# A chunked log-linear attention and gated FFN kernel: exponent rows in two fp16 parts, another order of the first transfers, and another list of due times

## The chip, the cores and the metric

One core of a Trainium2 chip runs the whole program. The metric is device time in microseconds (us), the median of several executions. Engines are called PE (TensorE, matmuls), DVE (VectorE), ACT (ScalarE), POOL (GpSimd) and SP (the queue from which all transfers are issued).

## The reference, cut to what matters

The input x is (2, 2048, 256), fp32: B = 2 sequences of T = 2048 tokens, D = 256. Layer 1 is attention with 16 heads of 64 key and 16 value dimensions, a decay and a level-dependent weight:

```
Q, K, V = x @ Wq.T, x @ Wk.T, x @ Wv.T;  dl = x @ Wdl.T        # 16 heads, 12 levels
g   = -exp(A_log) * softplus(x @ Wdt.T + dt_bias)
Lam = softplus(Lp * dl);  cg = cumsum(g, axis=time)
decay[t,s] = exp(cg[t] - cg[s])  for s <= t, else 0
lam[t,s]   = Lam[t, level(t,s)]   # level: 0 if s == t, else floor(log2(s xor t)) + 1
W = (Q K^T / 8) * decay * lam;   o = (W V) @ Wout.T + x
attention = layernorm(o) * ln_g + ln_b
x = layernorm(x + attention)
```

Layer 2 is a gated cell that runs over the two sequences as two time steps (c = f*c + i*g with sigmoid, sigmoid, tanh gates), with output h = tanh(x @ wo.T + c_final @ uo.T + bo); the result is layernorm(x + h).

## The kernel before

**Tiling.** The 2048 tokens are cut into 16 blocks of P = 128 (NC = 16); both sequences are handled in one pass over the blocks. Weights and activations are kept as two fp16 parts (names in `_h` and `_l`, or `xth`, `xtl`), so that a product takes three matmuls. For each block c:

- `load_x` brings the transposed block xt and makes xth (a cast) and xtl (the rest).
- `project` makes values, level weights and decays (pv, z, m, u, ln). `gp` holds g in parts; matmuls pc with `tri` and `ones` make its prefix sums. The logarithms of decay and level weight, 10 rows of 16 heads (LL), are split into parts in RP, transposed by PE (pt), copied out (RT), written to DRAM (scr, cg2) and read back as `Rb[b]` (tiles R0 and R1: rows of the query side) and `st[32:]` (rows of the key side, broadcast).
- `keys` makes Q and K (pqk, 8 groups of 12 matmuls), split into F (ACT) and L (DVE).
- `attend` makes the exponents by matmul: `arg = st.T @ Rb` sums, for each key and query, the right rows; ACT's exponential of it, DL, is decay times level weight. Scores sc are multiplied into DL on DVE, pi = DL.T @ V. What lies outside the block comes from up to four stored states (pin, SH, SL); pu and pS make the block's own state.
- `finish` runs po, two layernorms, a transpose (pt_x), the gates gt, pcu, ph, tanh, the last layernorm (hh) and the store. The last block (`fine`) does this one sequence at a time, with `warm` matmuls in between.

**Three bf16 parts.** Each exponent row is held as three bf16 numbers that sum to it: 30 rows, one for masked entries (-1e30) and an empty one make 32 rows a sequence, 64 in all with 16 heads (8 transposes of 128 columns). The arg matmuls contract 128 rows: 32 of indicators and query rows, 96 of the key side (2 x 48).

**The order of the work.** Every operation goes through a `Recorder`. `add` notes it with an estimated duration (`cost`); `depend` finds what each must wait for; `order` then plans: it steps through time with the estimated durations, numbers of buffers (`BUFS`) and of PSUM banks (`BANKS`), and on each engine starts, of the operations that are ready, the one with the earliest due time (`late`). `issue` emits the plan, and each engine runs its list strictly in that order. All instructions thus come from one line, L536, and are told apart by their tiles. Before, due times come from a due time for each block's output (`DUE`), followed backwards through the durations, plus a bias for each kind of operation (`BIAS`); `FIRST` names the first 16 transfers in order:

```
late[i] = min([outs.get(i, 1e9)] + [late[s] - ops[i].dur - ops[i].lat for s in succ[i]])
late = [x + bias.get(o.kind, bias.get(o.kind.split("@")[0], 0.0)) for x, o in zip(late, ops)]
late = [o.rank - 1e6 if o.rank >= 0 else x for x, o in zip(late, ops)]
```

Of the kernel before, what the change touches and what calls it, by code (L numbers as in the profile page):

```python
# [22 lines left out]
P = 128  # L23
# [3 lines left out]
NEG = -1e30  # L27
EPS = 1e-5
PERM = [3, 4, 5, 6, 7, 8, 9, 10, 11, 0, 1, 2]
SW = 64.0  # L30


DUE = [
    2677.57, 7721.13, 18978.35, 19716.23, 26604.1, 27450.81, 30772.73, 32390.67,
    34188.43, 36425.9, 37687.87, 40156.28, 43733.31, 46896.49, 47598.73, 59076.43,
]
BIAS = {
    'DVE:id16': -544.41, 'POOL:mhalf': -2585.45, 'POOL:ones': -884.87, 'POOL:RP': 1536.59, 'DMA:xt32@0': -4046.65,
    'DVE:xth@0': 1406.88, 'POOL:xtl@0': -518.54, 'DMA:xn@0': -2368.1, 'DMA:LpB@0': -3281.08, 'POOL:LpB@0': 860.85,
    'DVE:LpB@0': -244.97, 'DMA:bc_dtb@0': -2440.29, 'DMA:stg_wv@0': -6352.72, 'ACT:wv_h@0': -1203.55,  # L40
    'DVE:wv_l@0': 268.05, 'DMA:bc_Alog@0': -6629.31, 'ACT:bc_Alog@0': -1742.76, 'DVE:bc_Alog@0': -856.29,
    'DMA:mk@0': -4013.56, 'DMA:tri@0': -3595.99, 'DMA:stg_wq@0': -3921.89, 'ACT:wq_h@0': -1587.01,
    'DVE:wq_l@0': 1004.73, 'DMA:stg_wk@0': -4796.3, 'ACT:wk_h@0': 1541.09, 'DVE:wk_l@0': 3050.85,
    'DMA:st@0': -6284.79, 'DMA:R0@0': -6277.05, 'DMA:R1@0': -5991.07, 'POOL:SH@0': 665.45, 'POOL:SL@0': -2142.9,
    'POOL:VZ0@0': 1168.73, 'POOL:VZ1@0': -2626.46, 'PE:pv@0': -2541.05, 'DVE:z@0': -3273.44, 'ACT:VZ0@0': -4024.21,
    'POOL:z@0': -405.5, 'DVE:m@0': 572.33, 'ACT:u@0': 300.83, 'ACT:ln@0': 419.02, 'DVE:u@0': -1545.81,
    'ACT:LL@0': -482.21, 'POOL:g@0': -945.72, 'POOL:gp@0': 847.34, 'POOL:gr@0': 2525.08, 'PE:pc@0': -832.96,
    'POOL:LL@0': -1927.28, 'POOL:lf@0': -892.19, 'DVE:RP@0': 1443.6, 'DVE:r1@0': -759.26, 'PE:pt@0': -4539.93,
    'ACT:RT@0': -4433.14, 'DMA:scr@0': -628.34, 'DMA:cg2@0': -2529.67, 'POOL:E@0': -1904.15, 'ACT:E@0': -1974.72,
    'POOL:wv@0': 181.98, 'PE:pqk@0': 64.39, 'ACT:F@0': 1604.82, 'DVE:L@0': 240.14, 'DMA:bc_lng@0': 2134.89,  # L50
    'DMA:bc_lnb@0': -3284.28, 'DMA:bc_bo@0': 2756.69, 'DMA:ic@0': 2678.73, 'DMA:fb@0': 1506.14,
    'DMA:stg_wo@0': 214.04, 'ACT:wo_h@0': 749.49, 'DVE:wo_l@0': 13.57, 'DMA:stg_fw@0': 1917.56,
    'ACT:fw_h@0': -4483.73, 'DVE:fw_l@0': 3214.87, 'DVE:ich@0': 420.52, 'DVE:icl@0': -4538.93, 'PE:pg@0': 1562.45,
    'DVE:gb@0': 1718.11, 'PE:pu@0': 476.98, 'ACT:Uh@0': 2949.46, 'DVE:Ul@0': 1151.14, 'PE:pS@0': 1579.04,
    'ACT:N0@0': -3364.34, 'POOL:Ne0@0': -1812.42, 'POOL:Nt0@0': 2666.57, 'PE:arg@0': 1940.26, 'ACT:DL@0': 617.53,
    'PE:sc@0': 1032.21, 'DVE:DL@0': -2154.89, 'PE:pi@0': 14.24, 'ACT:YT@0': -2007.66, 'DVE:YTl@0': -1029.9,
    'ACT:SH@0': -122.62, 'DMA:xc@0': -943.46, 'PE:po@0': 1994.93, 'DVE:o@0': 25.16, 'POOL:xc@0': 1259.58,
    'DVE:st6@0': -1858.28, 'DVE:mv@0': -3427.79, 'POOL:rs@0': -1949.61, 'DVE:x1@0': -5553.71, 'PE:pt_x@0': -1400.7,
    'ACT:tr_x@0': -2328.9, 'DVE:tr_x@0': 2309.54, 'PE:gt@0': -1288.93, 'ACT:tg@0': -946.21, 'DVE:ct@0': -235.27,
    'DVE:c20@0': -3271.11, 'ACT:chh@0': -1127.08, 'DVE:chl@0': 554.25, 'DVE:c21@0': -872.21, 'PE:pcu@0': 3059.02,  # L60
    'DVE:cu@0': 1460.37, 'PE:ph@0': 1875.67, 'DVE:hh@0': -3488.44, 'ACT:hh@0': 132.07, 'POOL:hh@0': 3054.19,
    'DMA:out@0': 3049.1, 'DMA:xt32': -1810.23, 'DVE:xth': 64.72, 'POOL:xtl': -114.25, 'DMA:xn': -34.41,
    'PE:pv': -827.63, 'DVE:z': -1783.61, 'ACT:VZ1': -2672.79, 'POOL:z': 778.86, 'DVE:m': -789.82, 'ACT:u': 160.38,
    'ACT:ln': 591.53, 'DVE:u': 565.39, 'ACT:LL': 4374.65, 'POOL:g': 743.3, 'POOL:gp': -706.56, 'POOL:gr': 1663.66,
    'PE:pc': -2010.17, 'POOL:LL': 2926.67, 'POOL:lf': 3821.96, 'DVE:RP': -662.55, 'DVE:r1': -2759.89,
    'PE:pt': -165.69, 'ACT:RT': 659.27, 'DMA:scr': -1065.41, 'DMA:cg2': -986.92, 'DMA:st': 2349.73,
    'DMA:R0': -4459.06, 'DMA:R1': -920.98, 'POOL:E': 164.31, 'ACT:E': 3751.96, 'POOL:wv': -2316.25,
    'PE:pqk': 3231.38, 'ACT:F': 2373.65, 'DVE:L': 1459.54, 'POOL:ca': 2673.82, 'ACT:coef': 777.82,
    'PE:pu': 1486.59, 'ACT:Uh': -1034.21, 'DVE:Ul': -1341.83, 'PE:pS': -1300.83, 'ACT:N1': -1363.27,
    'POOL:Ne1': 3295.45, 'POOL:Nt1': -3412.65, 'POOL:mt': -860.48, 'POOL:N1': 1496.08, 'PE:arg': 10.51,  # L70
    'ACT:DL': -378.27, 'PE:sc': 1271.55, 'DVE:DL': 214.57, 'PE:pi': -1471.85, 'PE:pin': 557.54, 'DVE:Yi': 2234.51,
    'ACT:Yh': 1604.54, 'POOL:Yl': 569.07, 'ACT:YT': -714.54, 'DVE:YTl': -122.31, 'ACT:SH': 3886.77,
    'POOL:SL': -2249.79, 'DMA:xc': 1825.76, 'PE:po': -3323.98, 'DVE:o': -660.15, 'POOL:xc': -169.22,
    'DVE:st6': -348.25, 'DVE:mv': -2225.59, 'POOL:rs': 414.73, 'DVE:x1': -228.81, 'PE:pt_x': -545.23,
    'ACT:tr_x': -194.42, 'DVE:tr_x': 94.93, 'PE:gt': -1722.42, 'ACT:tg': -1182.38, 'DVE:ct': -4965.5,
    'DVE:c20': -807.68, 'ACT:chh': -2859.38, 'DVE:chl': -3393.25, 'DVE:c21': 92.69, 'PE:pcu': -3235.88,
    'DVE:cu': 958.49, 'PE:ph': 1685.23, 'DVE:hh': -2322.3, 'ACT:hh': -1393.34, 'POOL:hh': 1020.15,
    'DMA:out': -1687.37, 'ACT:VZ0': 887.84, 'ACT:N0': -1579.9, 'POOL:Ne0': 662.46, 'POOL:Nt0': 2273.86,
    'POOL:acc0': 1222.8, 'ACT:N2': 2274.54, 'POOL:Ne2': -1305.11, 'POOL:Nt2': 3789.98, 'POOL:N2': -2988.84,
    'DVE:tq': -1338.55, 'POOL:Yi': -418.52, 'POOL:acc1': -4347.71, 'ACT:N3': -1472.76, 'POOL:Ne3': -1671.15,  # L80
    'POOL:Nt3': -1206.59, 'POOL:N3': 747.56, 'DMA:xc@8': 15056.81, 'PE:po@8': 11984.32, 'DVE:o@8': 12872.18,
    'POOL:xc@8': 12701.25, 'DVE:st6@8': 9516.16, 'DVE:mv@8': 11273.9, 'POOL:rs@8': 13415.76, 'DVE:x1@8': 7496.93,
    'PE:pt_x@8': 12669.14, 'ACT:tr_x@8': 11859.29, 'DVE:tr_x@8': 8427.28, 'PE:gt@8': 10079.09,
    'ACT:tg@8': 16255.28, 'DVE:ct@8': 13065.88, 'DVE:c20@8': 12123.56, 'ACT:chh@8': 6769.1, 'DVE:chl@8': 13861.4,
    'DVE:c21@8': 9374.46, 'PE:pcu@8': 9104.07, 'DVE:cu@8': 14670.33, 'PE:ph@8': 10197.25, 'DVE:hh@8': 14713.5,
    'ACT:hh@8': 13013.82, 'POOL:hh@8': 17906.53, 'DMA:out@8': 8066.82, 'DMA:xt32@9': -3472.99,
    'DVE:xth@9': -6943.2, 'POOL:xtl@9': -7979.66, 'PE:pv@9': -7250.49, 'DVE:z@9': -7399.69, 'ACT:VZ1@9': -5093.65,
    'POOL:z@9': -8444.59, 'DVE:m@9': -3821.67, 'ACT:u@9': -8298.34, 'ACT:ln@9': -7589.28, 'DVE:u@9': -8544.13,
    'ACT:LL@9': -4666.75, 'POOL:g@9': -6445.41, 'POOL:gp@9': -525.04, 'POOL:gr@9': 1071.48, 'PE:pc@9': -5094.17,
    'POOL:LL@9': -7512.85, 'POOL:lf@9': -7085.42, 'DVE:RP@9': -8900.61, 'DVE:r1@9': -5745.08, 'PE:pt@9': -6171.97,  # L90
    'ACT:RT@9': -9289.92, 'DMA:scr@9': -5138.62, 'DMA:cg2@9': -12451.75, 'DMA:st@9': -8335.6, 'DMA:R0@9': -4913.0,
    'DMA:R1@9': -1320.23, 'PE:pqk@9': -5086.21, 'ACT:F@9': -2346.26, 'DVE:L@9': -4425.52, 'POOL:ca@9': -1966.77,
    'POOL:acc0@9': -4203.44, 'POOL:acc1@9': -2628.34, 'POOL:acc2@9': -6977.55, 'ACT:coef@9': -5726.39,
    'PE:arg@9': -8364.73, 'ACT:DL@9': -6371.85, 'PE:sc@9': -2442.58, 'DVE:DL@9': -5936.8, 'PE:pi@9': -8104.24,
    'PE:pin@9': -6842.43, 'DVE:Yi@9': -7958.54, 'DVE:tq@9': -4871.42, 'POOL:Yi@9': -9414.91, 'ACT:Yh@9': 923.7,
    'DVE:Yl@9': -13.59, 'ACT:YT@9': -5899.02, 'DVE:YTl@9': 948.32, 'DMA:xc@9': -3131.16, 'PE:po@9': -10407.06,
    'DVE:o@9': -6391.56, 'POOL:xc@9': -5874.17, 'PE:warm@9': 2241.77, 'DVE:st6@9': -3233.97, 'DVE:mv@9': -6158.55,
    'POOL:rs@9': -4272.53, 'DVE:x1@9': -8481.89, 'PE:pt_x@9': -10891.67, 'ACT:tr_x@9': -8747.79,
    'DVE:tr_x@9': -3011.58, 'DVE:b16@9': -459.04, 'PE:ph1@9': 2189.17, 'PE:gt0@9': -1044.0, 'ACT:tg@9': -4313.81,
    'DVE:ct@9': -4064.32, 'DVE:c20@9': -8811.46, 'ACT:chh@9': -9398.28, 'DVE:chl@9': -4364.2, 'PE:gt1@9': -8791.8,  # L100
# [1027 lines left out]
```

## Time and profile before

| what | value |
|---|---|
| median of 3 runs | 614.75 us (614.02 to 618.04) |
| the profiled execution | 615.93 us |
| its span, first to last instruction | 614.1 us |
| granted PE clock, mean | 0.991 |
| busy: PE, DVE, ACT, POOL | 585.6, 502.4, 383.4, 303.5 us |
| moved by DMA | 46.36 MB in 70139 packets |

The profile is one execution. An engine's busy time is the sum of its instructions' durations; PE's matmuls are pipelined, so they overlap and their modelled length is longer than the spacing at which they are issued. PEld is the loading of weights, beside the matmuls. A group's row gives the tiles (output <- input), the shape, the count, busy us, mean ns of one, and then the idle time ahead of it with what ended most of that. PEclk is the clock granted to PE in tenths: it was half until 13.2 us, for 3.4 us from 47.3, and at the very end.

### The profile page before, as it was taken

What the parts mean: (1) busy time and instruction counts of PE and PEld (TensorE: products, weight loads), DVE (VectorE), ACT (ScalarE), POOL (GpSimd) and SP (SyncE); (2) the same over time, 40 slices, a digit from 0 to 9 for tenths busy, and PEclk for the clock granted to TensorE, in tenths of its full rate; (3) what the DMA queues carried; (4) which work ended last, traced back from release to release, by engine and by line L of the source; (5) the groups of instructions that cost most, each with busy time, mean ns of one, the idle gap of its engine ahead of it and who ended that gap; (6) DMA issues with size and microseconds to landing.
All of it is one profiled execution on the core that took longest, in us unless ns stands there. A gap on an engine that the chain in (4) does not pass through costs nothing.

```text
span 614.1 us, 24206 instructions
## 1 busy us (share of the span) xinstructions
PE 585.6 (95%) x10382; PEld 504.2 (82%) x10382; DVE 502.4 (82%) x1196; ACT 383.4 (62%) x914; POOL 303.5 (49%) x666
## 2 busy tenths in 40 slices
PE   5988999999999999999999999999999999999894
PEld 2776788988898788978889888888988889888794
DVE  5977958888879997789786888897978879787974
ACT  4666587465784856558664674857467594664552
POOL 4461646134735729244772464547376455353432
PEclk9998999999999999999999999999999999999997
DMA  8785134311243205041411514114050512203001
GB/s 245 182 189 130 36 73 91 90 35 38 60 101 91 71 3 141 20 108 35 110 36 37 125 37 91 54 25 119 20 141 21 108 37 75 70 4 101 27 2 35
DMA packets 70139, 46.36 MB, mean 75 GB/s; under 512 B 23984, under 2 KB 67760, under 8 KB 70000
## 3 DMA queue, kind: packets, MB, share of 16 engines
q1 hardware_dynamic: 70032, 44.82, 29.3%
q8 instruction: 81, 1.33, 0.9%
q14 instruction: 26, 0.21, 0.1%
HBM read 35.63 MB, written 9.18 MB: 73 GB/s over the span
## 4 chain that ended last, share of the span: by engine, by line
PE 45%; DVE 23%; POOL 13%; ACT 9%; DMA 6%; issue 3%; SPq 0%; POOLq 0%; ACTq 0%; DVEq 0%
PE gt L536 10%; PE pqk L536 9%; PE pi L536 4%; PE sc L536 4%; POOL rs L536 3%; DVE DL L536 3%; PE ph L536 3%; DVE L L536 3%; ACT DL L536 3%; DVE m L536 3%; PE pv L536 3%; PE arg L536 2%; PE pin L536 2%; DVE st L536 2%; PE pu L536 2%
## 5 line engine op out<-in xcount | busy, mean ns | idle before, releaser
L536 PEld LDWEIGHTS <-fw_h 128*128 128x128 f16 x1176 | 90.9, 98 | 5.0 <-ACT fw_h L536 2.0
L536 ACT ACTIVATE F<-pqk 128x512 f16<-128x512 f32 x128 | 73.7, 616 | 30.3 <-PE pqk L536 28.5
L536 DVE SCALAR_TENSOR_TENSOR L<-pqk,F 128x512 f16<-128x512 f32 x128 | 82.6, 676 | 5.9 <-ACT F L536 5.9
L536 DVE SCALAR_TENSOR_TENSOR DL<-sc,DL 128x512 f32<-128x512 f32 x128 | 81.7, 677 | 4.8 <-PE sc L536 3.6
L536 PE MATMUL gt<-tr_x,fw_h 128*128 128x128 f16 x768 | 82.6, 219 | 0.3 <-DVE tr_x L536 0.2
L536 PEld LDWEIGHTS <-wk_h 128*128 128x128 f16 x992 | 69.9, 98 | 6.2 <-issue 0.6
L536 ACT ACTIVATE tg<-gt,gb 128x128 f32<-128x128 f32 x192 | 53.8, 373 | 33.9 <-PE gt L536 33.3
L536 ACT ACTIVATE DL<-arg 128x512 f32<-128x512 f32 x128 | 68.1, 616 | 6.8 <-PE arg L536 6.5
L536 PE MATMUL pqk<-xth,wq_h 128*128 128x256 f16 x256 | 70.1, 274 | 0.3 <-DVE o L536 0.3
L536 PE MATMUL gt<-tr_x,fw_l 128*128 128x128 f16 x384 | 70.0, 219 | 0.0
L536 PE MATMUL pqk<-xtl,wq_h 128*128 128x256 f16 x256 | 70.0, 273 | 0.0
L536 PE MATMUL pqk<-xth,wq_l 128*128 128x256 f16 x256 | 69.9, 273 | 0.0
L536 PEld LDWEIGHTS <-F 64*128 64x128 f16 x2048 | 60.8, 93 | 10.9 <-issue 8.4
L536 PE MATMUL pqk<-xth,wk_l 128*128 128x256 f16 x256 | 69.8, 272 | 0.0
L536 PE MATMUL pqk<-xth,wk_h 128*128 128x256 f16 x256 | 69.8, 272 | 0.0
L536 PE MATMUL pqk<-xtl,wk_h 128*128 128x256 f16 x256 | 69.7, 272 | 0.0
L536 PEld LDWEIGHTS <-fw_l 128*128 128x128 f16 x588 | 57.3, 98 | 1.8 <-DVE fw_l L536 1.0
L536 PEld LDWEIGHTS <-wq_h 128*128 128x128 f16 x512 | 48.6, 98 | 8.0 <-issue 0.7
L536 POOL TENSOR_TENSOR Yi<-Yi,tq 128x256 f32<-128x256 f32 x32 | 25.3, 791 | 49.2 <-DVE Yi L536 33.3
L536 PEld LDWEIGHTS <-wk_l 128*128 128x128 f16 x496 | 46.2, 98 | 4.1 <-issue 1.0
L536 PE MATMUL sc<-F 64*128 64x128 f16 x512 | 46.4, 218 | 0.3 <-DVE L L536 0.3
L536 PEld LDWEIGHTS <-L 64*128 64x128 f16 x1024 | 45.2, 93 | 0.7 <-issue 0.4
(179 smaller groups left out, 1809.7 us busy)
## 6 DMA issues: line engine op xcount, KB each, us to landing
st<-cg SPq DMA_DIRECT2D x16, 768.0 KB, 6.3
xt<-xT SPq DMA_DIRECT2D x16, 256.0 KB, 2.8
xc<-x SPq DMA_DIRECT2D x16, 256.0 KB, 2.8
scr<-RT SPq DMA_DIRECT2D x16, 256.0 KB, 2.9
R<-scr SPq DMA_DIRECT2D x32, 128.0 KB, 2.9
xn<-x SPq DMA_DIRECT2D x15, 256.0 KB, 3.2
out<-hh SPq DMA_DIRECT2D x15, 256.0 KB, 2.2
stg_fw<-fw SPq DMA_DIRECT2D x8, 256.0 KB, 3.7
```

Of the source, the lines that this page charges most:

```text
L536: getattr(eng.real, meth)(*[real(x) for x in a], **{q: real(x) for q, x in k.items()})
```

## The change

It has three parts.

1. *Exponent rows.* RP holds each row as two fp16 parts (20 rows a sequence, 5 transposes in place of 8). `g` is limited from below to -500 (one more POOL operation), split into two fp16 parts in place of three bf16 (4 pc matmuls in place of 6). Masked entries become 32768 x (-60000) through a constant row of `rc`. The DRAM copies shrink with it: cg2 has 32 rows a sequence in place of 48, st[32:96] is filled in place of st[32:128], R is read with 20 rows in place of 32, and arg contracts 96 rows in place of 128. st, R, tri, ones are fp16.
2. *The opening.* The first block's xth is made by ACT and xtl by DVE (before: DVE and POOL); wv arrives as two transfers of half the rows, each converted by itself. SP's first transfers are xt, wv (two), wq, wk, Lp, dtb, Alog, the second halves of wq and wk, tri, mk; before: xt, wv, wq, Lp, dtb, wk, Alog, tri, mk, the second halves.
3. *Due times.* `DUE`, `BIAS` and `FIRST` go. `PLAN` is a string with two characters for each recorded operation, its due time. BUFS, BANKS and some estimates of `cost` change with it. The whole order on every engine is new.

The core of the diff (PLAN's characters left out):

```diff
-NEG = -1e30
+NEG, GMIN = -60000.0, -500.0
...
-BANKS = {'y': 8, 'z': 8, 'x': 4, 'a': 7, 's': 5, 'p': 6, 't': 7,}
-FIRST = ["xt32", "stg_wv", "stg_wq", "LpB", "bc_dtb", "stg_wk", "bc_Alog", "tri", "mk", "xt32", "stg_wq", "stg_wk", "st", "R0", "R1", "xn"]
+BANKS = {'y': 7, 'z': 4, 'x': 4, 'a': 6, 's': 5, 'p': 4, 't': 6,}
...
             if sb > tb:
-                st[30, tb, s] = 1
+                st[20, tb, s] = 32768
                 continue
-            st[27:30, tb, s] = 1
+            st[18:20, tb, s] = 1
             row = (6, 7, 5, 8)[s % 4] if sb == tb else level(4 * tb, 4 * sb) - 3
-            st[3 * row:3 * row + 3, tb, s] = 1
+            st[2 * row:2 * row + 2, tb, s] = 1
...
-        late = [1e9] * n
-        for i in range(n - 1, -1, -1):
-            late[i] = min([outs.get(i, 1e9)] + [late[s] - ops[i].dur - ops[i].lat for s in succ[i]])
-        bias = BIAS
-        late = [x + bias.get(o.kind, bias.get(o.kind.split("@")[0], 0.0)) for x, o in zip(late, ops)]
-        late = [o.rank - 1e6 if o.rank >= 0 else x for x, o in zip(late, ops)]
+        base = len(DIGITS)
+        late = [DIGITS.index(code[2 * i]) * base + DIGITS.index(code[2 * i + 1]) - 200 for i in range(n)]
...
-                SP.dma_start(t, src)
-                act(hi[:, :, c0:c0 + w], t, AF.Copy, scale=SW)
-                V.scalar_tensor_tensor(lo[:, :, c0:c0 + w], t, SW, hi[:, :, c0:c0 + w], ALU.mult, ALU.subtract)
+                for ks in [slice(0, 1), slice(1, 2)] if name == "wv" else [slice(0, 2)]:
+                    SP.dma_start(t[:, ks], src[:, ks])
+                    act(hi[:, ks, c0:c0 + w], t[:, ks], AF.Copy, scale=SW)
+                    V.scalar_tensor_tensor(lo[:, ks, c0:c0 + w], t[:, ks], SW, hi[:, ks, c0:c0 + w], ALU.mult, ALU.subtract)
...
-            V.tensor_copy(xth, xt32)
-            G.tensor_tensor(xtl, xt32, xth, ALU.subtract)
+            if c == 0:
+                act(xth, xt32, AF.Copy)
+                V.tensor_tensor(xtl, xt32, xth, ALU.subtract)
+            else:
+                V.tensor_copy(xth, xt32)
+                G.tensor_tensor(xtl, xt32, xth, ALU.subtract)
...
+            G.tensor_scalar(g, g, GMIN, None, ALU.max)
-            gp, gr = work("gp", [3, B, H], BF16), work("gr", [B, H])
+            gp = work("gp", [2, B, H], F16)
             G.tensor_copy(gp[:, 0], g)
-            G.tensor_tensor(gr, g, gp[:, 0], ALU.subtract)
-            G.tensor_copy(gp[:, 1], gr)
-            G.tensor_tensor(gp[:, 2], gr, gp[:, 1], ALU.subtract)
+            G.tensor_tensor(gp[:, 1], g, gp[:, 0], ALU.subtract)
...
-                for q in range(3):
-                    PE.matmul(pc[:, 32 * j:32 * j + 32], w, gp[:, q].rearrange("p b h -> p (b h)"), start=(q == 0), stop=(q == 2))
+                for q in range(2):
+                    PE.matmul(pc[:, 32 * j:32 * j + 32], w, gp[:, q].rearrange("p b h -> p (b h)"), start=(q == 0), stop=(q == 1))
...
-            r1 = work("r1", [B, 10, H])
-            V.tensor_copy(RPv[:, :, :, 0, :], RF)
-            V.tensor_tensor(r1, RF, RPv[:, :, :, 0, :], ALU.subtract)
-            V.tensor_copy(RPv[:, :, :, 1, :], r1)
-            V.tensor_tensor(RPv[:, :, :, 2, :], r1, RPv[:, :, :, 1, :], ALU.subtract)
-            for q in range(8):
-                PE.transpose(pt[:, q, :], RP[:, q * P:(q + 1) * P], idb)
-            RT = work("RT", [8, P], BF16)
-            act(RT, pt, AF.Copy)
+            V.tensor_copy(RP[:, :, :, 0, :], RF)
+            V.tensor_tensor(RP[:, :, :, 1, :], RF, RP[:, :, :, 0, :], ALU.subtract)
+            for q in range(5):
+                PE.transpose(pt[:, q, :], RPf[:, q * P:(q + 1) * P], idh)
+            RT = work("RT", [5, P], F16)
+            act(RT, pt[:, 0:5, :], AF.Copy)
...
-            SP.dma_start(st[32:].rearrange("k (a d) t -> k a (d t)", d=2),
-                         cg2.rearrange("b k t -> (b k) t").unsqueeze(1).to_broadcast([96, 16, 2 * P]))
+            SP.dma_start(st[32:96].rearrange("k (a d) t -> k a (d t)", d=2),
+                         cg2.rearrange("b k t -> (b k) t").unsqueeze(1).to_broadcast([64, 16, 2 * P]))
...
-                SP.dma_start(Rb[b][:32].rearrange("k h t -> k (h t)"), rows[32 * b:32 * b + 32].rearrange("k h t -> k (h t)"))
+                SP.dma_start(Rb[b][:20].rearrange("k h t -> k (h t)"), rows[b].rearrange("k h t -> k (h t)"))
...
-                        PE.matmul(pa[:, :, 4 * j4:4 * j4 + 4], st[:, tb, :], Rb[b][:, :, 4 * tb:4 * tb + 4],
+                        PE.matmul(pa[:, :, 4 * j4:4 * j4 + 4], st[:96, tb, :], Rb[b][:96, :, 4 * tb:4 * tb + 4],
```

## The prediction

> **What bounds the kernel now.** I read the engine table and the slices first, then a table by stages, then TensorE's waits, then the opening and the single groups that the change touches. All sums are made against the profiled execution: span 614.1 us, 615.93 us with what lies around it, 1.2 us above the median of 614.75.
>
> ```profile
> PE 585.6 (95%) x10382; PEld 504.2 (82%) x10382; DVE 502.4 (82%) x1196; ACT 383.4 (62%) x914; POOL 303.5 (49%) x666
> ...
> PE   5988999999999999999999999999999999999894
> ...
> PEclk9998999999999999999999999999999999999997
> ```
>
> TensorE (PE) is the bound for some 570 us; what it does not do is idle at both ends and in slices 2 to 4. VectorE (DVE) at 82% is no bound, but close enough that a late operation there stalls PE. By stages (columns: length, then busy us and instructions of PE, weight loads, DVE, ACT, POOL; clock; DMA):
>
> ```profile
> 0.00:12.30 12.30, 4.82 (x13) 1.73 (x14) 6.30 (x7) 5.27 (x7) 7.05 (x18) 1.00 0.77 236
> 12.30:30.00 17.70, 17.20 (x174) 13.82 (x173) 16.09 (x32) 11.70 (x25) 7.21 (x22) 1.00 0.78 198
> 30.00:60.00 30.00, 25.61 (x430) 20.79 (x432) 22.37 (x43) 18.05 (x41) 12.31 (x29) 0.94 0.71 167
> 60.00:584.00 524.00, 515.79 (x9495) 447.87 (x9486) 439.29 (x1063) 337.06 (x808) 268.26 (x581) 1.00 0.27 66
> 584.00:614.20 30.20, 22.15 (x289) 20.02 (x286) 18.38 (x55) 11.34 (x36) 8.70 (x17) 0.88 0.06 19
> ```
>
> Busy time flatters PE, because a matmul's modelled length (0.219 us for 128 columns) is four times its spacing in a stream (0.056). So I also took spacings from the trace: 0.109 us for 256 columns, 0.056 for 128, 0.029 for 64, 0.0265 for 32, and 0.095 extra wherever PE goes between whole-array matmuls and the half-height (sc, pin) or quarter-width (pi) ones. What exceeds the spacings I call lost: 11 us before 30, 7.3 from 30 to 60, 14.6 from 60 to 584, and some 10 after. The 14.6 are many short stalls; the largest are of the exponent matmuls arg:
>
> ```profile
> PE arg L536 <- DVE L L536: 2.3, 6, 0.8
> PE pS L536 <- DVE mv L536: 0.7, 1, 0.7
> PE pi L536 <- POOL Yl L536: 0.6, 1, 0.6
> ```
>
> By spacings, 5.8 of the 14.6 us stand in front of an arg group (3.6 between two arg groups, 2.2 between a pqk and an arg group). A group of eight takes PE 0.23 us, its exponential 0.6 us on ACT: PE runs out of banks when such groups are bunched.
>
> **The PE stream.**
>
> ```profile
> L536 PE MATMUL pt<-idb,RP 128*128 128x128 bf16 x128 | 9.8, 220 | 0.7 <-DVE z L536 0.5 <-DVE L L536 0.2
> L536 PE MATMUL arg<-R,st 128*128 128x64 bf16 x1024 | 41.6, 192 | 4.0 <-DVE L L536 2.3 <-ACT DL L536 0.8
> L536 PEld LDWEIGHTS <-st 128*128 128x128 bf16 x1024 | 38.2, 97 | 8.1 <-issue 6.7
> L536 PEld LDWEIGHTS <-L 64*128 64x128 f16 x1024 | 45.2, 93 | 0.7 <-issue 0.4
> ```
>
> Transposes pt go from 8 to 5 a block: 48 x 0.056 = 2.7 us less. Prefix matmuls pc go from 6 to 4: 32 x 0.0265 = 0.8 us less. In the instruction order of the two built programs, changes of array shape rise from 163 to 184: 21 x 0.095 = 2.0 us more. Stream: -1.5 us (range -3.5, if the changes fall into stalls, to -0.5).
>
> The 1024 arg matmuls keep their 64 columns, but contract 96 rows instead of 128, in fp16. No row has 96 rows. Low bound: a load with 64 rows takes 93 ns against 97 with 128, and fp16 streams at the spacing of bf16, so nothing. High bound: each takes the 0.056 us of a 128-column matmul, 1024 x 0.027 = +27.6 us. I take nothing, since 96 rows lie between two heights that behave alike. The Trainium skill, "TensorE: Matmul & The Clock Gate", section "LDWEIGHTS (loading the stationary operand)", says that loading time follows the columns and not the rows; by it the term is nothing too, and no run here shows 96 rows.
>
> **Other engines, per block.** DVE loses a cast and a subtraction around r1 (0.390 + 0.551 us by their groups): 15 us in all. ACT's copy RT shrinks from 1024 to 640 columns (1.03 to about 0.65 us): 6 us; table loads go from 28 to 24 at 1.283 us: 5.1 us. POOL swaps a cast and a subtraction (0.23 + 0.25) for one tensor_scalar (0.36 by Nt's row): 2 us. DMA: the broadcast into st falls from 768 to 512 KB, scr from 256 to 160, the two R loads from 128 to 80 each: 0.45 MB a block. None of it is PE time; the cover is PE's own queue. With the cover gone, the path from m to the first arg would be 1.5 us shorter, which pays only where PE stands waiting for it.
>
> **The opening.**
>
> ```profile
> 3.58 2.26 DVE L536 CAST xth<-xt 128x512 f16<-128x512 f32 x1 [1.92 <-DMA xt<-xT]
> ...
> 15.56 0.43 DVE L536 CAST xth<-xt 128x512 f16<-128x512 f32 x1 [0.24 <-DMA xt<-xT]
> ```
>
> The first cast needs 0.43 us and took 2.26, beside POOL's memsets. PE's second matmul then waits for xtl on POOL, at 8.04 us, and runs gapless from there; pv ends at 12.27. Now ACT casts (0.65 us by wo_h's row, also 512 columns from SBUF): xth at 4.2. DVE subtracts: 0.7 us if POOL leaves it alone, until the memset ends near 5.1 and then 0.7 if not; xtl at 5.0 to 5.8. wv comes in halves; the first wv_l follows after 0.57 us, at 5.6 to 6.4, and the other ten pv matmuls at the cold 0.39 us end pv at 9.5 to 10.3: 2.0 to 2.8 us earlier. (The skill's page "SBUF — State Buffer", section "SBUF: two separate sides", has a two-input VectorE operation blocked only by a GpSimd operation that reads SBUF, which a memset does not; by it pv ends at 9.5, but no row shows that pair.) Then the wq halves are late: wq lands at 8.4 as before (its bytes still follow xt and wv), wq_l is done at 10.7 and wk_l near 12.4, behind LpB and z on DVE, while PE now comes to them at 10.4 and 11.7, because it takes wk for the first pair right after wq, where before it had 12 wq matmuls more to do. Those stalls are new, 0.4 and 0.7 us, and later ones 0.2. Opening: -2.4 + 1.3 = -1.0 us (range -2.8 to +0.5). SP's queue issues wq, wk and their second halves ahead of LpB, tri and mk; those small ones are wanted after 10 us and land in time.
>
> **30 to 60 us.** Here pg waits for the gate weights (1.8 + 0.9 us), and the half clock of one 3.4 us window follows (1.7 us). fw's sixth slice was issued at 36.46 and landed 9.5 us later, with the DMA engines full. Now pg stands as one piece behind pt, five more pqk pairs and pv. From the earlier pt (about 27.5) that is 14.7 us of PE work: it is reached at 42. The slice has 0.45 MB less before it, some 2 us at 210 GB/s, but is now queued on SP behind both R loads: there at 41.5 to 44. I take a loss of 5.5 us for 7.3: -1.8 (range -5 to +2).
>
> **60 to 584 us.** The new due times spread the evictions. Laying both orders out at the spacings above: places where six evictions of pqk or arg come within 3.0 us of PE work (six take ACT 3.0 us) fall from 113 to 34; three arg groups within 1.8 us fall from 57 to 25. The span of a block's eight arg groups grows from 4.1 us to 10, with pqk between. Against it, a few fillers became shorter than the chains that they cover: from pt_x to its first gate 0.3, 1.6 and 1.8 us in three blocks where 1.9 was the least, and the chain through ACT and DVE takes 1.0 to 1.8. I take two thirds of arg's 5.8 us back, -4.0, and +1.0 for the short fillers, and -0.5 for pc's 2.1 us of stalls, one POOL step shorter: -3.5 (range -9 to +4).
>
> **The tail.** From the last block's first po (583.97) to the end are 30.1 us, of which 19.3 are PE work. In the new order the last gates of block 14 stand ahead of that po, so 17.3 us of work are left behind it; the chain through two layernorms, gates and output loses their company on ACT and DVE, about 1.8 us. Work moved ahead, +2.0 against -1.8: 0 (range -2 to +3).
>
> **Sum:** -1.5 - 1.0 - 1.8 - 3.5 + 0 = -7.8 us: 608.1 by the profiled execution, 607.0 by the median. I forecast 607.0, with 602 to 612 as its own range.
>
> **Rivals.**
> *The stalls only move* (chance 0.22). DVE stays at 80% in strict order; whatever operation is late there stops PE elsewhere. For: the waits are scattered over 12 pairs, and many short slots changed. Against: the fall in bunches. Then only stream, opening and half of 30 to 60 remain: 614.75 - 3.4, about 611.5.
> *The stalls mostly go* (0.15). If two thirds of the 14.6 and 5 of the 7.3 us vanish: 614.75 - 1.5 - 2.0 - 5 - 9.7 = 596.5 to 602.
> *Slower: the 96-row arg matmuls lose their spacing* (0.08). Place: every arg group; price 27.6 us at worst: 634.5. It outweighs the other terms once each arg takes 7.8 / 1024 = 7.6 ns more than 29. Against it: both neighbouring heights.
>
> **How the numbers follow.** Forecast 0.55. The 8-in-10 range reaches from the better rival to no gain at all: 599 to 614.5. This kernel's measurement can tell about 1% from no change: below 608.6 lie all of the better rival and 0.4 of the forecast's 0.55, so faster 0.55; between 608.6 and 620.9 the rest of the forecast, the moved stalls and a small loss of spacing: 0.38; above it 0.07.
>
> **What would show it.** pt x80 and pc x64 at the old lengths; arg x1024 spaced at 0.029 us and its weight loads near 97 ns; PE's second matmul before 6 us and pv's end near 10; the half-clock window near 47 us gone or smaller; PE's idle time between 60 and 584 down from 8.2 us to about 5, with the waits of arg the ones that shrink; the last po some 28 us before the end. I am wrong if PE's idle time between 60 and 584 is not smaller, or if arg's spacing is over 0.036.

## The result, and the profile after

| | median, us | runs | before, measured beside it | ratio (95%) |
|---|---|---|---|---|
| kernel after | 617.47 (614.94 to 620.16) | 20 | 615.74 | 1.0032 (1.0018 to 1.0046) |

The change gains nothing; it costs some 2 us. The prediction was 607.0 with a range from 599 to 614.5. The page of the profiled execution of after, first the busy times, then PE's and its clock's slices:

```profile
PE 584.7 (95%) x10302; PEld 502.4 (82%) x10302; DVE 491.1 (80%) x1166; ACT 379.4 (62%) x912; POOL 294.1 (48%) x647
...
PE   6798999999999999999899999899999999999994
...
PEclk9987999999999999999999999999999999999998
```

By the same stages as before (length, busy and instructions of PE, weight loads, DVE, ACT, POOL; clock; DMA):

```profile
0.00:12.30 12.30, 6.79 (x27) 3.26 (x28) 6.14 (x12) 6.06 (x9) 5.13 (x16) 1.00 0.69 237
12.30:30.00 17.70, 13.90 (x151) 11.12 (x149) 13.69 (x25) 9.75 (x21) 7.63 (x20) 1.00 0.77 196
30.00:60.00 30.00, 27.98 (x417) 22.80 (x416) 23.70 (x42) 19.20 (x43) 10.56 (x28) 0.83 0.46 131
60.00:584.00 524.00, 513.12 (x9374) 444.57 (x9367) 428.09 (x1034) 333.89 (x809) 260.50 (x565) 1.00 0.18 53
584.00:614.60 30.60, 22.96 (x356) 20.61 (x353) 19.52 (x58) 10.46 (x30) 10.29 (x19) 0.94 0.06 19
```

PE does 2 us more than before up to 12.3 us, and then 3.3 us less up to 30 us. In the third stage the clock is 0.83 instead of 0.94: half speed from 30.9 to 34.3 and from 51.3 to 58.2 us, where before had one window, from 47.3 to 50.7. The same columns for the two windows of after:

```profile
30.90:34.30 3.40, 3.40 (x14) 2.34 (x13) 3.35 (x5) 2.85 (x7) 0.89 (x1) 0.50 0.21 67
51.30:58.20 6.90, 6.82 (x124) 5.67 (x123) 5.21 (x10) 3.99 (x9) 0.15 (x1) 0.51 0.47 140
```

I read the difference as a running account: each matmul that PE has issued so far counts with its spacing from the prediction, and the time that has passed less this work is what PE has lost by then. From the profiles:

| lost up to, us | 20 | 35 | 50 | 60 | 584 | end |
|---|---|---|---|---|---|---|
| before | 10.4 | 11.0 | 16.2 | 18.4 | 33.0 | 42.5 |
| after | 8.3 | 14.3 | 15.9 | 20.1 | 35.8 | 44.6 |

A lead of 2.1 us at 20 us is a lag of 3.3 at 35. Where it goes is in PE's waits and in ACT's order of time (start, duration, instruction; in brackets the idle time before it and what ended it):

```profile
25.61 0.36 PE L528 MATMUL pv<-wv_h,xth 128*128 128x464 f16 x1 [1.26 <-ACT LL L528]
...
29.37 1.13 PE L528 MATMUL pu<-wv,xn 128*128 128x256 f32 x4 [2.42 <-POOL wv L528]
```

```profile
20.49 0.59 ACT L528 ACTIVATE F<-pqk 128x512 f16<-128x512 f32 x1
24.55 0.63 ACT L528 ACTIVATE wo_h<-stg_wo 128x512 f16<-128x512 f32 x1 [3.47 <-DMA stg_wo<-wo]
25.09 0.36 ACT L528 ACTIVATE VZ<-pv 128x256 f32<-128x256 f32 x1
25.35 0.21 ACT L528 ACTIVATE LL<-pc 128x64 f32<-128x64 f32 x1
...
25.97 0.23 ACT L528 ACTIVATE E<-LL 128x32 f32<-128x32 f32 x1
```

pc is done at 21.6 us. Its eviction LL stands in ACT's strict queue behind wo_h, which waits 3.47 us for weights that are wanted much later. PE waits for LL's bank, then for E and wv, which follow from LL. Before, wo_h ran without a wait:

```profile
22.64 0.65 ACT L536 ACTIVATE wo_h<-stg_wo 128x512 f16<-128x512 f32 x1
```

### The profile page after: what moved, and what is told of

Its sections match the earlier page's. It is cut to its first block, busy times and chain, and to the rows that moved or that the text cites. A ratio compares the mean times of both kernels' runs of the same rounds, so it can differ in the third digit from the quotient of the medians.

```text
span 614.6 us, 23993 instructions
## 1 busy us (share of the span) xinstructions
PE 584.7 (95%) x10302; PEld 502.4 (82%) x10302; DVE 491.1 (80%) x1166; ACT 379.4 (62%) x912; POOL 294.1 (48%) x647
## 4 chain that ended last, share of the span: by engine, by line
PE 62%; DVE 14%; POOL 11%; issue 5%; ACT 4%; DMA 3%; SPq 1%; POOLq 0%; ACTq 0%; DVEq 0%
PE pqk L528 16%; PE gt L528 13%; PE sc L528 5%; PE pi L528 5%; PE pu L528 3%; POOL rs L528 3%; PE pv L528 3%; PE arg L528 3%; PE ph L528 3%; PE pS L528 3%; PE pin L528 3%; PE po L528 2%; DVE L L528 2%; DVE st L528 2%; DMA stg_wo<-wo 2%
## 5 line engine op out<-in xcount | busy, mean ns | idle before, releaser
L528 ACT ACTIVATE F<-pqk 128x512 f16<-128x512 f32 x128 | 75.7, 601 | 43.9 <-PE pqk L528 42.8
L528 DVE SCALAR_TENSOR_TENSOR L<-pqk,F 128x512 f16<-128x512 f32 x128 | 85.3, 680 | 10.7 <-ACT F L528 10.0
L528 DVE SCALAR_TENSOR_TENSOR DL<-sc,DL 128x512 f32<-128x512 f32 x128 | 83.4, 680 | 6.2 <-PE sc L528 4.9
L528 ACT ACTIVATE tg<-gt,gb 128x128 f32<-128x128 f32 x192 | 56.7, 368 | 39.1 <-PE gt L528 38.0
L528 ACT ACTIVATE DL<-arg 128x512 f32<-128x512 f32 x128 | 71.4, 606 | 11.2 <-PE arg L528 10.9
L528 PEld LDWEIGHTS <-F 64*128 64x128 f16 x2048 | 62.3, 94 | 13.7 <-issue 11.3
L528 PE MATMUL sc<-F 64*128 64x128 f16 x512 | 48.1, 221 | 0.6 <-DVE DL L528 0.2
L528 PE MATMUL sc<-F,L 64*128 64x128 f16 x512 | 47.3, 219 | 0.3 <-issue 0.3
L528 PE MATMUL arg<-R,st 96*128 96x64 f16 x1024 | 44.0, 193 | 3.6 <-ACT DL L528 1.4
```

What stands on the lines that cost most here:

```text
L528: getattr(eng.real, meth)(*[real(x) for x in a], **{q: real(x) for q, x in k.items()})
```

## The experiments

An order is written out as a list in these kernels, so that one part can change and the rest stay. Medians stand beside the median of before in the runs measured with them. The ratio to before that follows is not that of the two medians, and can differ from it by up to 1 us; where it reads otherwise, both are given.

**1. wo_h moved back** on ACT, in after (DVE's wo_l and fw_l follow):

```diff
-F, wo_h, VZ, LL<-pc, fw_h, E, E, F, VZ
+F, VZ, LL<-pc, E, E, F, wo_h, fw_h, VZ
```

> The kernel after, with ScalarE's wo_h and first fw_h (and VectorE's wo_l and fw_l) moved behind LL<-pc, the two E and one F, nothing else. Theory Q (ScalarE's queue): the lead of 2.1 us that PE has at 20 us is lost because VZ, LL<-pc and E stand behind wo_h, which waits 3.5 us for its weights; the two PE stalls at 24.1 and 26.6 us (1.5 + 2.6 us) go, and with them the half clock from 30.9 to 34.3 us (1.7 us): 617.5 - 5.8 = about 612 (611 to 614); if the gate weights at pg are then late, up to 615. Rival M (the many short stalls of the new order between 60 and 584 us): what is won before 60 us is lost again later, 616.5 to 617.5.

Measured 614.10 (before 615.57), ratio 0.9988 (0.9974 to 1.0003): 3.4 us better than after, not 5.8. The two stalls and the half clock at 30.9 go. But a stall of 2.0 us comes at 33 us, where PE waits for DVE's L, which stands behind a late fw_l: part of the lateness moved from ACT's queue to DVE's. The gain stayed through to the end (by the ratios it is 2.7 us), against rival M.

**2. The two parts alone**, in the order of before:

```diff
 RP, gp, pt, RT, scr, cg2, st, R   # as in after
-load_x, load_w, order as in after
+load_x, load_w, order as in before
```

> The kernel before, in its own order of instructions, with the exponent rows in two fp16 parts only (the operations that fall away are taken out where they stood; the clamp of g stands ahead of gp). Theories Q and M agree: 48 transposes and 32 prefix matmuls less, 3.5 us, and no change of array shape more: 615.7 - 3.5 = about 612 (610.5 to 613.5). Rival P (the two parts themselves cost something, for instance in the 96-row matmuls): 616 or more. By stages: if the loss by spacings between 60 and 584 us stays at 14.6 us, the work taken from VectorE, ScalarE and GpSimd is worth nothing there; at 12 or less it is.

Measured 614.67 (615.57), ratio 0.9998 (0.9980 to 1.0015): 0.9 us better by the medians and no better by the ratio, where all theories but P had 3.5. ACT waited 2.5 us at wo_h here too, in the very order of before, and with fewer bytes ahead of it. So neither the new order nor the number of bytes made stg_wo late; something in the two parts did.

```profile
25.54 0.63 ACT L576 ACTIVATE wo_h<-stg_wo 128x512 f16<-128x512 f32 x1 [2.50 <-DMA stg_wo<-wo]
```

**3. The stall filled**, in after, in front of the first pu of block 0:

```diff
+for _ in range(24):
+    PE.matmul(pu[:, 0, :], Wq[0][:, 0, :P], Wk_[0][:, 0, :256], start=True, stop=True)
```

> The kernel after with 24 matmuls more of 256 columns on PE in front of the first pu of block 0, into pu's own bank, which pu then overwrites: they fill the stall at 26.6 us (24 x 0.109 = 2.6 us) with work and change no wait. Theory Q says that the stall is what brought the half clock from 30.9 to 34.3 us: that window goes, the stall stays, 617.5 - 1.7 = about 615.8. If the window does not hang on the stall: 617.5, with the half clock where it was.

Measured 615.45 (615.57), ratio 1.0014 (0.9995 to 1.0032): with more work 2.0 us better than after by the medians. By the ratios it is 1.1, and the two intervals overlap, so the size is not settled. In the profile the half clock from 30.9 to 34.3 us is gone; the next one is from 49.7 to 56.6. So the stall cost twice in after: its own time and the slow window behind it.

**4. stg_wo earlier**, in after, by SP's order alone:

```diff
-xt, st, R0, R1, xn, stg_wo, stg_fw, fb
+xt, xn, stg_wo, stg_fw, st, R0, R1, fb
```

> The kernel after with the transfers of st and of both R (864 KB, wanted after 40 us) issued behind stg_wo and the first stg_fw instead of ahead of them; no engine's order but SyncE's changes. Theory Q: stg_wo lands some 4 us earlier (864 KB at about 210 GB/s), near 20.5 us, ScalarE does not stand at wo_h, and the gain is that of the run with wo_h moved: about 612 (611 to 614). Rival M: 616.5 to 617.5. If the DMA engines are not what makes stg_wo late, it lands at 24.5 as before and nothing changes.

Measured 613.35 (615.57), ratio 0.9970 (0.9952 to 0.9988): 4.1 us better than after, faster than before. wo_h runs at 21.6 without a wait.

What is new ahead of stg_wo in runs 2 and after is the two transfers of R's constant rows: 76 rows of 4 KB each where before has 96. The Trainium skill, "DMA: Bandwidth & Descriptors", section "Why a DMA increments its semaphore by 16 and not by 1", says that a transfer runs on the largest number of engines up to 16 that divides the size of the outermost dimension on both sides, here the count of rows. For 76 that is 4. The next four runs test it.

**5. 80 rows instead of 76**, in after:

```diff
-SP.dma_start(Rb[b][20:96].rearrange("k h t -> k (h t)"), A["rc"][b])
+SP.dma_start(Rb[b][16:96].rearrange("k h t -> k (h t)"), A["rc"][b])
```

> The kernel after; the constant rows of each R are loaded as 80 rows (16 to 95) instead of 76 (20 to 95), the four more being overwritten by R's own rows later; all orders stay. Theory R (row count): the two 76-row transfers are slow by themselves. In the trace of after their 152 packets of 4 KB start over 8.1 us (13.7 to 21.8 us), in that of before 192 such packets over 4.0 us (13.5 to 17.5); everything behind them, stg_wo too, comes late by that. With 80 rows stg_wo lands near 21, SyncE does not stand 5.1 us at xc, ScalarE does not wait at wo_h: 617.5 - 4.5 = about 613 (611.5 to 614.5), as with wo early. Rival (only the place of stg_wo behind so many bytes counts, 16 KB more each make it worse by 0.1 us): 617.5.

Measured 613.03 (615.87), ratio 0.9953 (0.9941 to 0.9965): 4.4 us better than after, by moving 32 KB more. SP had stood at the issue of xc in after, and wo_h had waited; with 80 rows the issue takes 0.54 us and wo_h does not wait. First after, then this run:

```profile
15.67 5.10 SPq L528 DMA_DIRECT2D xc<-x  x1
```

```profile
17.97 0.54 SPq L576 DMA_DIRECT2D xc<-x  x1
...
22.65 0.63 ACT L576 ACTIVATE wo_h<-stg_wo 128x512 f16<-128x512 f32 x1
```

**6. The two parts alone, 80 rows**, the same edit in run 2:

> The run with the two parts in the order of before, with 80 constant rows instead of 76. In the 76-row run ScalarE waited 2.5 us for stg_wo and PE 2.1 us at 26.4 and 28.8 us, which before does not. Theory R: both go, 614.7 - 2.5 = about 612 (610.5 to 613), which is the 3.5 us of stream against before. Rival (the two parts' own cost is elsewhere): 614.7.

Measured 611.99 (615.87), ratio 0.9932 (0.9915 to 0.9949): 3.9 us faster than before. This is what the two parts are worth.

**7. 76 rows in the kernel before**, nothing else:

```diff
-SP.dma_start(Rb[i][32:]..., A["rc"][i])
+SP.dma_start(Rb[i][32:108]..., A["rc"][i][:76])
+SP.dma_start(Rb[i][108:]..., A["rc"][i][76:])
```

> The kernel before, unchanged but for this: each 96-row load of constant rows into R goes as two transfers, of 76 and of 20 rows. The same bytes, two issues more on SyncE (0.4 us each). Theory R: stg_wo lands 3 us later, ScalarE waits at wo_h (none before), PE stalls near 25 to 29 us: 615.6 + 2.5 = about 618 (617 to 619.5). Rival: 615.6 to 616.2, the two issues.

Measured 619.67 (615.87), ratio 1.0063 (1.0051 to 1.0075): 3.8 us slower with the same bytes, and the wait appears:

```profile
26.46 0.63 ACT L655 ACTIVATE wo_h<-stg_wo 128x512 f16<-128x512 f32 x1 [4.06 <-DMA stg_wo<-wo]
```

**8. The transfers alone:**

```diff
+for n, r in enumerate((96, 80, 76, 72, 64, 32, 20) * 2):
+    nc.sync.dma_start(t[:r], A["src"][:r])
+    nc.vector.tensor_copy(res[:r, 0, n:n + 1], t[:r, 0:1])
```

> A kernel of its own, which computes nothing of the reference: transfers of 96, 80, 76, 72, 64, 32 and 20 rows of 4 KB from HBM to SBUF, twice, each alone (the next waits until VectorE has read of the one before). Theory R: the 76-row transfer takes at least 2 us longer than the 80-row one, though it is 16 KB smaller. Rival: times go with the bytes, 76 rows a little under 80. By the Trainium skill, page DMA: Bandwidth & Descriptors, section Why a DMA increments its semaphore by 16 and not by 1, a transfer runs on the largest number of engines up to 16 that divides its row count: 16 for 96, 80, 64 and 32, 12 for 72, 10 for 20, and 4 for 76, which would put 76 near four times the length of 80.

In order of time (the number in brackets is how long VectorE waited for the transfer; r80x is the tile of 80 rows; the last line is the second transfer of 96 rows):

```profile
12.81 0.15 DVE L24 CAST res<-r80x 80x1 f32<-80x1 f16 x1 [3.24 <-DMA r80x<-src]
...
18.08 0.15 DVE L24 CAST res<-r76x 76x1 f32<-76x1 f16 x1 [5.12 <-DMA r76x<-src]
...
21.58 0.15 DVE L24 CAST res<-r72x 72x1 f32<-72x1 f16 x1 [3.35 <-DMA r72x<-src]
...
33.23 0.15 DVE L24 CAST res<-r96x 96x1 f32<-96x1 f16 x1 [3.22 <-DMA r96x<-src]
```

76 rows take 5.12 and 5.21 us, 80 rows 3.24 and 2.96, 72 rows 3.35 and 3.36: the slow one is neither the largest nor the smallest. Run 7's 76 rows start at row 32 of the tile and run 8's at row 0, so it is not the start at row 20 that makes 76 slow.

The trace does not say on which engines the packets ran, but from their starts and lengths one can count how many are under way at once. For 76 rows it is 4 during 2.9 of 3.9 us (3.3 of 4.0 the second time), and never more than 6. The count held longest is 15 for 96 rows, 14 for 80, 16 for 64, 13 for 32 (which are over in 0.7 us), 11 or 12 for 72, and 10 for 20 rows. By the page's rule the engines are 16 for the first four, 12 for 72, 10 for 20 and 4 for 76, so the counts agree with it closely. From first packet to last, 76 rows take 3.9 us against 1.6 for 80, 2.4 times and not the four times that I had worked out from the page: on the mean, 10.3 to 10.6 packets of the 80 rows are under way, not 16, and 3.8 to 3.9 of the 76. It is the same inside the kernels: in after, the 152 packets of the constant rows start over 8.5 us with 3.9 under way on the mean, in before 192 over 5.1 us with 9.6 (these are all the packets; the 8.1 and 4.0 us in what was expected of run 5 are a little short).

**9. Less work on DVE**, on run 5 (the low part of k is left out of the scores):

```diff
-V.scalar_tensor_tensor(L[:, :, :, i4, :], pq, 0.25, hi, ...)
+V.scalar_tensor_tensor(L[:, 0, :, i4, :], pq[:, 0], 0.25, F[:, 0, :, i4, :], ...)
-for ti, (k_, q_) in enumerate(((F, F), (L, F), (F, L))):
+for ti, (k_, q_) in enumerate(((F, F), (F, F), (F, L))):
```

> The run with 80 rows in the order of after; VectorE computes the low parts L of q only, not those of k, and the score matmuls that read k's low part read F instead (this part of the computation is left out; PE's work and every order stay). VectorE loses 128 x 0.26 us (a spacing of 0.60 for 512 columns to about 0.34 for 256) = 33 us, from 80% to 75%. Theory D (the stalls between 60 and 584 us come from VectorE's load): the loss by spacings there falls from 15.6 to 11 or less, 613.0 - 4.5 = about 608.5. Theory O (they come from the fixed order, in which a PE operation stands right behind a short chain; no engine is short of time): it falls by 1.5 at most, 611.5 to 613.

Measured 611.18 (615.13), ratio 0.9928 (0.9903 to 0.9953). DVE is busy 462.4 us instead of 490.9, and the loss between 60 and 584 us is 15.6 as in run 5. That the two are equal is chance: this profile has a half-clock window from 392.8 to 396.2 us, run 5's has none there, and 3.4 us at half clock cost 1.7 at most. Without it the loss would be 13.9 or more, 1.7 less at most; theory D had 11 or less, theory O a fall of 1.5 at most. The 1.9 us come from before 60 us (14.8 lost instead of 17.4; 1.6 of it by 20 us, where the second half of wv landed earlier, which the edit does not touch). So the load of DVE is not what makes most of those stalls.

**10. The three repairs together**, in the order of after (edits of runs 1, 4 and 5):

> The order of after with the three repairs together: 80 rows, wo_h behind LL, E and F on ScalarE, st and R issued behind stg_wo and stg_fw. The 80-row run alone has 613.0 and loses 17.4 us up to 60 us, with stalls of 0.6 at 27 and 0.8 at 34 us left. If the repairs add up: 611.5 (610.5 to 612.5). If they all cure the one late transfer: 613.

Measured 612.68 (615.13), ratio 0.9959 (0.9944 to 0.9975). They do not add up (0.4 us better than run 5 by the medians, 0.4 worse by the ratios), as they would not if all three cure the same late transfer.

**11 and 12. The opening of after in front of the order of before**, both with the two parts and 80 rows; run 11 also issues st and R later, as run 4:

```diff
-order: before
+order: after up to 18 us of its plan, then before
```

> As the run with the order of before, the two parts and 80 rows (612.0), but with the opening of after (its first 18 us). It measures what the opening is worth alone. From the losses up to 20 us (before 10.4; in four runs with the opening of after 8.3, 9.2, 9.3 and 9.9, the second half of wv landing at different times): 1.2 on the mean, 612.0 - 1.2 = about 611 (610 to 612). If the opening is lost again at the stalls that follow at 26 to 28 us: 612.

> The order of before with the two parts and 80 rows, the opening of after (its first 18 us: the casts on ScalarE and VectorE, wv in halves, the order of the first transfers, and PE's order of the first pqk), and st and R issued behind stg_wo and stg_fw. The run without opening and without the later st and R has 612.0; opening 1.0 (below), stalls at 26.4 and 28.2 us 1.5: 609.5 (608.5 to 611).

Run 12 measured 610.88 (615.13), ratio 0.9924 (0.9902 to 0.9947): the fastest kernel of all by its median. Run 11 measured 611.45, ratio 0.9929 (0.9905 to 0.9952): later st and R bring nothing once no transfer is slow; the miss is mine, the stalls at 26 and 28 us were already gone in run 12.

## Why the prediction was wrong, step by step

The runs take the change apart:

| step | us, by medians | us, by the ratios | from |
|---|---|---|---|
| two fp16 parts, rows in a good number | -3.9 | -4.2 | run 6 against before |
| the opening | -1.1 | -0.5 | run 12 against run 6 |
| the new due times behind the opening, with their buffers and banks | +2.1 | +1.8 | run 5 against run 12 |
| 76 rows | +4.4 | +4.9 | after against run 5 |
| sum | +1.5 | +2.0 | measured +1.7, by the ratio +2.0 |

From the intervals, the first and the last step are known to about 1 us and the two between to about 1.7, because the median of before beside them was 615.87 once and 615.13 once. So the time of the opening alone is not told from nothing.

**The stream: right.** pt x80 and pc x64 at the old lengths; PE's work by spacings went from 571.6 to 570.0 us, -1.6 for -1.5, and run 6, which has the transposes and prefix matmuls without the added changes of shape, gained 3.9 for 3.5. The work is 568.0 in run 12 and 570.0 in run 5, but the 2.0 between them are the count of changes of shape times the assumed 0.095, no measurement; what the trace of after does show is that the middle one of its 184 changes adds 0.096 us, as in before. Whether they are most of the +2.1 of the new due times is not shown: between 30 and 60 us, where run 12 has no half clock, run 5 also loses 1.8 more. **The 96-row matmuls: right.** By form:

```profile
L528 PE MATMUL arg<-R,st 96*128 96x64 f16 x1024 | 44.0, 193 | 3.6 <-ACT DL L528 1.4 <-DVE L L528 1.1 <-issue 1.0
L528 PEld LDWEIGHTS <-st 96*128 96x128 f16 x1024 | 39.5, 97 | 7.4 <-issue 4.9 <-DVE L L528 0.2
```

193 ns for 192, 97 for 97, and the median spacing of arg is 0.029 us in both traces. That rival is out.

**The opening: right in size by the account, and its end was the end of what I followed.** (The sum as written, -2.4 + 1.3, is -1.1.) PE's second matmul is at 5.13 us, pv ends at 9.79; of the new stalls, PE waited 0.5 us for wk_l (forecast 0.7). Up to 20 us, nine profiles with the new opening lost 8.3 to 9.9 us (mean 8.9), four with the old one 9.8 to 10.7 (mean 10.2): -1.3 for -1.0. The spread is the second half of wv, which lands at different times. The Trainium skill's rule that a two-input VectorE operation is blocked only by a GpSimd operation that reads SBUF ("SBUF — State Buffer", section "SBUF: two separate sides") had no row in the trace of before. The trace of after has one, and it agrees: POOL cleared SL until 4.32 us and SH from 4.25 to 5.20, and xtl began at 4.20, right behind xth, and was not held up.

```profile
3.37 0.95 POOL L528 MEMSET SL<- 128x1024 f16 x1
4.25 0.95 POOL L528 MEMSET SH<- 128x1024 f16 x1
```

```profile
4.20 0.69 DVE L528 TENSOR_TENSOR xtl<-xt,xth 128x512 f16<-128x512 f32 x1 [0.93 <-ACT xth L528]
```

**The failed step: "DMA: ... the two R loads from 128 to 80 each: 0.45 MB a block. None of it is PE time".** I priced transfers by bytes, looked at the steady blocks only, and named PE's own queue as cover. The constant rows, loaded once, went from 96 to 76 rows, fewer bytes and 2 us longer each; and at 14 to 25 us there is no cover, since ACT's queue carries the late weights ahead of what PE needs. For the first transfers I asked only whether the small ones land in time, and never laid ACT's queue past 12 us beside the transfers that it waits for. Price: +4.4 where the sum had nothing. It falls between 20 and 60 us, where after lost 11.8 us and run 5 lost 7.5. Of the 9.5 us between the forecast -7.8 and the measured +1.7, these are 4.4, and the stage from 60 to 584 us is another 4.6 (+1.1 for -3.5). Without the 76 rows the time is 613.03, inside the range that was given and 6 us above the forecast.

**30 to 60 us: half right.** I had a loss of 5.5 for 7.3; it was 7.6 in after, 6.5 in run 5, 4.7 in run 12. PE's wait at pg did shrink, from 2.7 us before to 0.8, and it is no longer for the gate weights:

```profile
PE pg L536 <- ACT fw_h L536: 1.8, 1, 1.8
...
PE pg L536 <- DVE fw_l L536: 0.9, 2, 0.5
```

```profile
PE pg L528 <- DVE L L528: 0.8, 1, 0.8
```

But the half clock that I had tied to that wait did not go with it. All seven profiles with the new order have a window of 3.4 or 6.8 us that begins between 48.1 and 51.3 us, while runs 2, 6, 11 and 12, with the order of before and the two parts, have none there. What in the order brings it is open.

**60 to 584 us: wrong.** Forecast -3.5; PE's idle time went from 8.2 to 10.9 us, the loss from 14.6 to 15.7, and by the test that I had set ("I am wrong if PE's idle time between 60 and 584 is not smaller") this part fails by itself. The bunches did go: stretches of over 8 us in which ACT never pauses for 0.1 us fell from 7 to 2. In front of arg, the loss fell from 5.8 to 3.4 us, 2.4 of the 4.0 counted on. But others grew by 3.5: the largest new ones are four within 10 us near 400, where pv, pt and gt wait for banks that DVE has to clear or tiles that it makes (3.8 us in all, at the same place and of nearly the same size in every run with this order). The rival "the stalls only move" holds in this stage. That fewer bunches mean fewer stalls was the wrong inference. 29 us less work on DVE shorten the sum by 1.7 at most (run 9), and the 10 us less that the two parts take from it in the old order do not shorten it (run 6: 16.2 for 14.6); what would is open. That each stall is a short chain in the fixed order fits this, but no run shows it.

**The tail: right.** The last block's first po is 27.9 us before the end (forecast 28; before 30.1), and the loss from 584 us on is 8.8 for 9.5.

The largest rival, 611.5, was nearest and still too fast: no case of mine had a transfer that grows longer as it gets smaller.

## What to carry to other kernels

Look at the row count of every transfer that a change resizes, not only at its bytes: 80 rows cost less time than 76. When the first part of a kernel is made faster, follow each strict queue beyond it, and ask of every operation that waits for a transfer what stands behind it. Evening out the bursts on one engine is no gain by itself; it has to be read from the waits of the engine that bounds.

## What the runs showed of the hardware that was not expected

- A 76-row transfer of 4 KB rows took 5.1 to 5.2 us alone, 72, 80 and 96 rows 3.0 to 3.4. Of the 76 rows, 4 packets were under way at once for most of the time; of 96, 80 and 64 rows it was 14 to 16 for the longest.
- In after, an issue behind two such transfers held SP's queue for 5.10 us; with 80 rows the same issue took 0.54. That the queues of the few engines in use were full is my reading; the trace shows only the time.
- 24 matmuls that compute nothing, put into a stall, made the kernel 1 to 2 us faster: the half clock that had followed the stall did not come.
